# All four scatters of a slot wait for the last product of the next slot

## The chip, the core and the metric

The kernel runs on one core of a Trainium2 chip. The metric is the time of the whole program on the device, in microseconds (us), with everything between the inputs in HBM and the output in HBM. The core has five engines that run side by side, each through its own queue of instructions in order: TensorE (PE, matrix products; its weight loads are listed as PEld), VectorE (DVE), ScalarE (ACT), GpSimd (POOL) and SyncE (SP). Engines wait for each other through counters (semaphores): one engine raises a counter when an instruction is done, another waits until it has a certain value. SP here only issues transfers; POOL issues the indirect ones.

## The reference

One layer of a graph network with a residual and a layer norm, in float32:

```
x: 6250 x 128;  edges e = 0..99999, sorted by dst[e];  W: 384 x 128
h[e]   = concat(x[src[e]], x[dst[e]], edge_attr[e]) @ W + b
h[e]   = relu((h[e] - mean) / sqrt(var + 1e-5) * gamma + beta)
agg[n] = sum of h[e] over all edges with src[e] == n
out    = layernorm(x + agg)
```

The edges arrive sorted by `dst`, while the sum goes over `src`.

## The kernel before, in words

The 100,000 edges are cut into 782 tiles of 128 edges. Four tiles make a *slot* `q` (196 slots, loop at L1118). The kernel has two halves that overlap.

The first half computes, for each slot in the order of `dst`, the part of `h` that comes from the edge attributes and from `x[dst]`. `edges(s, q)` (L602) does it on PE: four products in float32 of the attributes with their weights (L611), then four products in bf16 that pick the `dst` rows out of a window of 42 nodes (L615); all go to one PSUM bank `hp`, of which there are two. `evict` (L619) copies the bank to SBUF on ACT, to one of eight buffers `hs` (L623), with the local number of the source node beside it (L624). Then POOL scatters each of the slot's four tiles to HBM with one indirect transfer (L641): every row of 128 values goes to its place in `sorted`, where the edges stand by blocks of source nodes. The places `place_i` were computed by counting, in work spread over earlier slots (`places`, L438).

The second half reads `sorted` back by pairs of blocks and adds the `x[src]` part, normalises and sums. The edges are divided into six splits (L38); a split is read back once all its scatters have landed, while the next split's slots run. A pair (class `Pair`, L719) passes through steps in fixed places of a flow (`FLOW`, L1063): SP loads it (`hl`, L715); DVE compares for the one-hot matrix (L733); PE turns that (L745) and ACT copies it (`ohn`, L749); ACT copies the loaded rows into PSUM (`sel`, L755); PE adds the picked rows of `x` to them (`pick`, L772); ACT squares and sums (L781) and takes the root (L784); DVE takes the reciprocal (L790) and scales (L796); PE sums by node (L805), and DVE adds that to the accumulator (L810). The last split is done by the class `Unit` (L819) after all slots, with the final layer norm.

The order on PE, DVE, ACT and SP is the order of the Python code (manual schedule, L973). In a slot it is: the loads for later slots, `edges(s, q)`, one step of the flow, `evict(s, q)`, a piece of `places`, the remaining steps of the flow, and then the scatters of the slot before. POOL's order is left to the scheduler of the framework; in the middle of the kernel POOL has nothing but scatters.

The scatters of slot `q - 1` are called at the end of slot `q` (L1144). From slot 13 to slot 194 they are *tied*: beside the wait for their `hs` buffer they wait for certain products of PE in slot `q`. For this, `pe()` (L99) notes the products of the slot as they are written, with their cost in columns (4 for float32, 1 for bf16): those of `edges`, of the turn, the pick and the sums, but not those of `places`. `scatters` (L630) then walks through the list and takes four of them: the products at which a quarter, a half, three quarters and all of the slot's cost are reached. Scatter `k` waits for the `k`-th of them. The scatters of the first 12 slots and of the last two are not tied.

Of the kernel before, what the change touches and what calls it, by code (L numbers as in the profile page):

```python
# [84 lines left out]
def fast_path(ctx, tc, io, bad_d, found):  # L85
# [10 lines left out]
    written = mybir.DependencyInfo(mybir.DependencyClass.Sync, mybir.DependencyReason.DATA)  # L96
# [91 lines left out]
    iota_p, zero_p, at = beside[:, 0:P], beside[:, P:P + 1], beside[:, P + 8:P + 8 + NB]  # L188
# [441 lines left out]
    def scatters(n, tied):  # L630

        total, seen, at = sum(c for _, c in done), 0, []
        for i, c in done:
            seen += c
            while len(at) < n and seen * n >= (len(at) + 1) * total:
                at.append(i)
        done.clear()
        for k, (s, q, j) in enumerate(waiting[:n]):
            t = q * PT + j
            parts = P if t < TILES - 1 else LAST  # L640
            i = nc.gpsimd.indirect_dma_start(  # L641
                out=sorted_d[s][:, :],
                out_offset=bass.IndirectOffsetOnAxis(ap=place_i[:parts, t:t + 1], axis=0),
                in_=hs_all[q % HS][:parts, j, :], in_offset=None,
            )
            if tied:
                tc.add_manual_dep(i.ins, at[k].name, written, reason="rows behind products")
            tc.declare_no_dep(i.ins, group=f"scatter{s}", reason="rows of different edges")
            tc.add_to_no_dep_group(f"scatter{s}", i.ins)
            if q < EARLY:  # L650
                tc.declare_no_dep(i.ins, group="clear", reason="see check_early")
                tc.add_to_no_dep_group("early", i.ins)
        del waiting[:n]
# [461 lines left out]
    for s, (n_tiles, _, _, _) in enumerate(SPLITS):  # L1115
        p0, p1 = first_tile[s] // PT, -(-first_tile[s + 1] // PT)
        slots = p1 - p0
        for i in range(slots):  # L1118
# [19 lines left out]
            if not TIE[0] <= q < TIE[1]:  # L1138
                scatters(len(waiting), False)
# [3 lines left out]
            if TIE[0] < q < TIE[1]:  # L1143
                scatters(len(waiting) - PT, True)  # L1144
# [359 lines left out]
```

## Time and profile before

| | |
|---|---|
| runs | 1376.14 us median of 3 (1372.72 to 1377.86) |
| the profiled execution | 1380.69 us, its span 1378.9 us |
| granted clock of PE, mean | 0.857 |
| PE | 975.2 us busy (71%) |
| DVE | 855.0 us busy (62%) |
| ACT | 773.5 us busy (56%) |
| POOL | 798.9 us busy (58%), of which 782 scatters 760.4 us |
| DMA | 247 MB, 179 GB/s over the span |

The span is the time from the first to the last instruction of the profiled execution. A row of the timeline begins with its start and its length in us; a bracket tells how long the engine had been idle before it and what ended that ("issue": nothing that the profile shows; "remote": a signal whose sender it can't name). A row of the groups by line has the busy time, the mean duration in ns, and the idle time before it. Starts and ends of matrix products are partly modelled, and a scatter's duration on POOL is that of its issue, not of the transfer.

### The profile page before, as it was taken

The numbers are of one execution on the slowest core, as the hardware profiler recorded it, in microseconds if no ns is written. First come the engines' busy times: TensorE is split into PE (matmuls) and PEld (weight loads), VectorE is DVE, ScalarE is ACT, GpSimd is POOL, SyncE is SP. The second block draws the span as 40 slices with busy tenths as digits, with TensorE's granted clock in tenths as the row PEclk, the third lists the DMA queues.
The fourth block names the chain that finished last, engine by engine and source line by source line (L and its number), as shares of the span: only waits on it lengthen the run. The fifth ranks groups of instructions, "written<-read, shape, count | busy, mean of one in ns | idle before, by whom it ended". The sixth has DMA issues, their size and how long they took to land. (4 is left out here: it accounts for less than half of the span.)

```text
span 1378.9 us, 27543 instructions
## 1 busy us (share of the span) xinstructions
PE 975.2 (71%) x8886; PEld 870.3 (63%) x8886; DVE 855.0 (62%) x2376; ACT 773.5 (56%) x3118; POOL 798.9 (58%) x835
## 2 busy tenths in 40 slices
PE   7457464345767676778777677778778787876895
PEld 5445453334666665777676667777778776765674
DVE  8573434524465656556575657678688867554797
ACT  4223232112555655564565557676778788665796
POOL 3656666666566665666565666566555555556054
PEclk9768687666888989878888899999999999988898
DMA  7758586455666655556656555665667655543332
GB/s 223 236 168 255 171 241 204 142 154 155 184 199 210 199 158 163 178 157 198 207 171 200 172 184 178 208 208 187 190 193 227 183 181 171 170 140 100 112 122 72
DMA packets 128052, 247.22 MB, mean 179 GB/s; under 512 B 47005, under 2 KB 61231, under 8 KB 127897
## 3 DMA queue, kind: packets, MB, share of 16 engines
q1 hardware_dynamic: 101924, 191.92, 46.8%
q0 software_dynamic: 25104, 53.05, 11.0%
q8 instruction: 71, 1.16, 0.4%
q14 instruction: 83, 0.68, 0.2%
q10 hardware_dynamic: 870, 0.40, 0.1%
HBM read 155.49 MB, written 89.80 MB: 178 GB/s over the span
## 5 line engine op out<-in xcount | busy, mean ns | idle before, releaser
L641 POOL DMA_INDIRECT sorted<-hs,place_i x782 | 760.4, 972 | 498.1 <-issue 210.6
L772 PE MATMUL sel<-xa,ohn 128*128 128x128 bf16 x2550 | 214.3, 232 | 174.9 <-issue 78.5
L781 ACT ACTIVATE sq<-sel 128x128 f32<-128x128 f32 x850 | 224.2, 280 | 158.9 <-PE sel L772 58.2
L772 PEld LDWEIGHTS <-ohn 128*128 128x128 bf16 x2550 | 174.8, 104 | 204.4 <-issue 174.7
L611 PE MATMUL hp<-w,eT 128*128 128x128 f32 x1564 | 258.3, 314 | 51.2 <-issue 37.9
L611 PEld LDWEIGHTS hp<-w,eT 128*128 128x128 f32 x1564 | 234.3, 225 | 83.2 <-issue 59.3
L805 PE MATMUL pa<-msg,ohe 128*128 128x130 f32 x1700 | 259.2, 308 | 24.1 <-issue 14.9
L623 ACT COPY hs<-hp 128x512 f32<-128x512 f32 x196 | 114.2, 583 | 288.7 <-issue 97.7
L805 PEld LDWEIGHTS pa<-msg,ohe 128*128 128x128 f32 x1700 | 236.4, 217 | 32.2 <-issue 19.0
L796 DVE SCALAR_TENSOR_TENSOR msg<-sel,rstd,cut 128x128 f32<-128x128 f32 x850 | 240.7, 345 | 8.0
L781 ACT ACTIVATION_READ_ACCUMULATOR sq<-sel 128x1 f32 x850 | 178.8, 210 | 0.0
L810 DVE TENSOR_TENSOR acc<-acc,pa 128x260 f32<-128x260 f32 x125 | 53.0, 424 | 201.0 <-PE pa L805 57.9
L733 DVE TENSOR_TENSOR ohe<-hl,beside 128x1024 f32<-128x1024 f32 (+2 forms) x125 | 131.4, 1052 | 23.3 <-PE sel L772 14.6
L749 ACT COPY ohn<-tr 128x1024 bf16<-128x1024 bf16 (+2 forms) x125 | 109.5, 876 | 37.9 <-PE pa L805 14.7
L755 ACT COPY sel<-hl 128x512 f32<-128x512 f32 (+1 forms) x225 | 127.9, 569 | 1.8 <-DVE msg L796 1.0
L599 DVE TENSOR_SCALAR ohd<-db,part_w 128x512 bf16<-128x512 bf16 x192 | 69.7, 363 | 72.1 <-remote 50.9
L615 PE MATMUL hp<-win,ohd 126*128 126x128 bf16 x782 | 88.5, 236 | 17.4 <-issue 15.4
L790 DVE RECIPROCAL rstd<-std 128x4 f32<-128x4 f32 (+1 forms) x225 | 38.6, 171 | 96.7 <-ACT std L784 45.2
L615 PEld LDWEIGHTS <-ohd 126*128 126x128 bf16 x782 | 69.0, 108 | 25.2 <-issue 20.9
L745 PE MATMUL tr<-ident_h,ohe 128*128 128x128 bf16 x850 | 75.5, 230 | 11.1 <-issue 9.4
L784 ACT ACTIVATE std<-ss,eps 128x4 f32<-128x4 f32 (+1 forms) x225 | 66.9, 297 | 7.3
L745 PEld LDWEIGHTS <-ohe 128*128 128x128 bf16 x850 | 57.7, 103 | 14.3 <-issue 14.2
(198 smaller groups left out, 1043.4 us busy)
## 6 DMA issues: line engine op xcount, KB each, us to landing
eT<-in_eT SPq DMA_DIRECT2D x96, 512.0 KB
hl<-sorted SPq DMA_DIRECT2D x75, 528.0 KB
db<-drel_d SPq DMA_DIRECT2D x96, 256.0 KB
sorted<-empty SPq DMA_DIRECT2D x100, 198.0 KB
hl<-sorted SPq DMA_DIRECT2D x50, 264.0 KB
sorted<-hs,place_i POOLq DMA_INDIRECT x782
hl<-sorted SPq DMA_DIRECT2D x25, 396.0 KB
sorted<-empty SPq DMA_DIRECT2D x50, 132.0 KB
```

The source lines that it names most:

```text
L611: pe(nc.tensor.matmul(hp[:, j, :], eT[:, at], w[:, 2, :], start=j == 0, stop=False, skip_group_check=True), 4)
L615: pe(nc.tensor.matmul(hp[:, j, :], oh[:3 * WN, at], win[:3 * WN, :], start=False, stop=j == m - 1, skip_group_check=True))
L623: nc.scalar.copy(hs[:, :m, 0:D], hp[:, :m, :])
L641: i = nc.gpsimd.indirect_dma_start(out=sorted_d[s][:, :], out_offset=bass.IndirectOffsetOnAxis(ap=place_i[:parts, t:t + 1], axis=0), in_=h ...
L733: nc.vector.tensor_tensor(self.ohe[:, :k, :], self.hl[:, :k, D:D + 1].to_broadcast([P, k, P]), row_bc(iota_p, k), op=ALU.is_equal)
L745: pe(nc.tensor.transpose(tr[:, j, :], half[:, j0 + j, 1::2], ident_h))
L749: nc.scalar.copy(self.ohn[:, :self.k, :], self.tr[:, :self.k, :])
L755: nc.scalar.copy(self.sel[g][:, :m, :], self.hl[:, j0:j0 + m, 0:D])
L772: pe(nc.tensor.matmul(sel[:, j, :], self.ohn[:, j0 + j, :], xa[:, b, i * D:(i + 1) * D], start=False, stop=j == m - 1 and i == 2, skip_gro ...
L781: nc.scalar.activation(sq[:, j, :], self.sel[g][:, j, :], AF.Square, accum_out=ss[:, j:j + 1])
L796: nc.vector.scalar_tensor_tensor(self.msg[:, j0 + j, 0:D], self.sel[g][:, j, :], rstd[:, j:j + 1], cut, op0=ALU.mult, op1=ALU.max)
L805: pe(nc.tensor.matmul(self.pa[:, h, :], self.ohe[:, j, :], self.msg[:, j, :], start=(j == h), stop=(j == k - 2 + h)), 4)
```

## The change

```
             if tied:
-                tc.add_manual_dep(i.ins, at[k].name, written, reason="rows behind products")
+                tc.add_manual_dep(i.ins, at[-1].name, written, reason="rows behind products")
```

Each of the four tied scatters of a slot now waits for the last product in the list, instead of the first for the product at a quarter, the second for that at a half, and so on. The last scatter waits for what it waited for before. In the built program, only the first of the four carries a wait for PE. The order of the instructions on PE, DVE, ACT and SP is the same as before. On POOL the scatters stand in the same order but for the last ten: the tied scatters of slot 193 stood mixed with those of slot 194, and now stand as a block of four behind the first three of slot 194. PE's products that raise its counter go from 1618 to 1086, since a product raises it only where something waits for it.

## The prediction

> **What bounds the kernel now.** I read the page first, then POOL's rows stage by stage, because the change touches POOL alone.
>
> ```profile
> span 1378.9 us, 27543 instructions
> PE 975.2 (71%) x8886; PEld 870.3 (63%) x8886; DVE 855.0 (62%) x2376; ACT 773.5 (56%) x3118; POOL 798.9 (58%) x835
> L641 POOL DMA_INDIRECT sorted<-hs,place_i x782 | 760.4, 972 | 498.1 <-issue 210.6
> ```
>
> No engine is full over the span. The 782 scatters take 760.4 us of POOL and leave 498.1 us of gaps between them. The table by stretches (columns: stretch, length, busy POOL time with the number of scatters, granted clock, DMA share, GB/s) gives the pace of a slot, which has four scatters:
>
> ```profile
> 100.00:275.00 175.00, 110.08 (x114) 0.73 0.68 204
> 275.00:540.00 265.00, 164.91 (x170) 0.83 0.57 178
> 540.00:810.00 270.00, 164.82 (x171) 0.83 0.58 180
> 810.00:1005.00 195.00, 117.42 (x121) 0.93 0.63 197
> 1005.00:1265.00 260.00, 145.41 (x151) 0.93 0.58 174
> ```
>
> Length over count times four: 6.14, 6.24, 6.32, 6.45 and 6.89 us a slot. POOL alone needs less. Its rows in time order show scatters back to back every 1.27 us (0.97 busy, 0.30 between), so 5.1 us a slot, and a longer gap where it waits. The waits of POOL in the last four stretches (in total us, times, longest) count those back-to-back gaps:
>
> ```profile
> POOL sorted L641 <- issue: 49.0, 124, 2.4
> POOL sorted L641 <- issue: 40.6, 118, 1.8
> POOL sorted L641 <- issue: 28.7, 77, 1.8
> POOL sorted L641 <- issue: 31.6, 76, 3.1
> ```
>
> What is left are stops: 170 - 124 = 46, then 53, 44 and 75, or 1.08, 1.24, 1.45 and 1.99 stops per four scatters. So POOL is close to setting the pace, and the question is why the others do not run ahead of it. The timeline of the last scatters, which are tied to nothing and run from 1263.10 to 1274.57 without a stop, shows it:
>
> ```profile
> 1263.10 0.97 POOL L641 DMA_INDIRECT sorted<-hs,place_i  x1 [0.40 <-issue]
> ...
> 1268.55 2.09 PE L805 MATMUL pa<-msg,ohe 128*128 128x130 f32 x8 [1.06 <-issue]
> ...
> 1274.57 0.87 POOL L641 DMA_INDIRECT sorted<-hs,place_i  x1 [0.30 <-issue]
> 1277.58 0.59 ACT L749 COPY ohn<-tr 128x512 bf16<-128x512 bf16 x1 [4.56 <-remote]
> 1277.70 0.43 DVE L810 TENSOR_TENSOR acc<-acc,pa 128x260 f32<-128x260 f32 x1 [7.93 <-remote]
> ...
> 1278.71 1.44 PE L772 MATMUL sel<-xa,ohn 128*128 128x128 bf16 x12 [8.07 <-ACT sel L755]
> ...
> 1285.25 0.43 DVE L810 TENSOR_TENSOR acc<-acc,pa 128x260 f32<-128x260 f32 x1 [0.18 <-PE pa L805]
> ...
> 1288.32 0.43 DVE L810 TENSOR_TENSOR acc<-acc,pa 128x260 f32<-128x260 f32 x1 [0.18 <-PE pa L805]
> ```
>
> PE finished the sums for DVE at 1270.64, and DVE got them at 1277.70, 2.3 us after the last scatter's end (1274.57 + 0.87); ACT's copy waited 4.56 us for an earlier product, and PE itself stood idle for 8.07 us behind ACT. Once the scatters are over, the same handover takes 0.18 us. So while scatters follow each other, the signal by which PE tells ACT and DVE of a finished product is **held**; it comes out in a stop of POOL. The same in the early stretch, timeline of slot 41:
>
> ```profile
> 259.92 0.39 PE L615 MATMUL hp<-win,ohd 126*128 126x128 bf16 x4
> ...
> 265.62 0.97 POOL L641 DMA_INDIRECT sorted<-hs,place_i  x1 [0.30 <-issue]
> ...
> 272.48 0.59 ACT L623 COPY hs<-hp 128x512 f32<-128x512 f32 x1 [13.52 <-issue]
> ...
> 273.12 2.08 PE L611 MATMUL hp<-w,eT 128*128 128x128 f32 x8 [12.82 <-ACT hs L623]
> ```
>
> ACT waits 13.52 us for a product that was done at 260.31, and PE 12.82 us for ACT. What one stop costs POOL, in mid-kernel:
>
> ```profile
> 639.42 0.97 POOL L641 DMA_INDIRECT sorted<-hs,place_i  x1 [0.30 <-issue]
> ...
> 641.70 0.96 POOL L641 DMA_INDIRECT sorted<-hs,place_i  x1 [1.30 <-PE hp L615]
> ```
>
> From the start of the last scatter of a row to the start of the next one it is 2.28 us instead of 1.27. That is the shortest kind of stop: the signals come out, and POOL goes on with them.
>
> **The change part by part.** No instruction of PE, DVE, ACT or SP moves, and no DMA is added or taken away.
>
> Removed: three of the four ties of a slot. Counted in the two built programs, 532 of PE's 1618 products that raise its counter no longer do, and POOL's queue has some 540 separate wait instructions fewer. A scatter that follows another takes 1.27 us from start to start in the untied run above as in the tied one, so the waits cost POOL nothing by themselves: 0.
>
> Added: the first scatter of a slot now waits for the last product of the next one. Behind it on POOL's queue stand only scatters, up to the tail. Who waits for those: ACT, to reuse the `hs` buffer eight slots later, some 50 us at 6.3 us a slot; and SP's first load of a sorted stretch.
>
> ```profile
> 279.15 1.00 POOL L641 DMA_INDIRECT sorted<-hs,place_i  x1 [0.30 <-issue]
> ```
> ```profile
> 297.48 0.00 SPq L715 DMA_DIRECT2D hl<-sorted  x1
> ```
> ```profile
> 1281.71 0.32 SPq L831 DMA_DIRECT2D hl<-sorted  x1
> ```
>
> The last scatter of the first split starts at 279.15, the load that needs it at 297.48. A scatter can slip by three back-to-back steps, 3.8 us; 18 us cover that: 0. At the end the last scatter starts at 1274.57 and the load that needs it at 1281.71. POOL's order of the last ten changes too: four tied ones now stand behind three untied ones, and may stop POOL once more. Between 0 and 3.8 us; half, 2 us.
>
> Moved: the stops. A slot is now four scatters in a row and one stop, with at least 3 x 1.27 + 2.28 = **6.09 us**, provided that PE has got through its whole slot when its signals come out. That is the lower end. In the five stretches it is worth -0.05, -0.15, -0.23, -0.36 and -0.80 us a slot. With 28.5, 42.5, 42.75, 30.25 and 37.75 slots that is -1, -6, -10, -11 and -30: **-58 us**.
>
> The other end: PE, ACT and DVE hand work to and fro inside a slot, and every handover from PE made during the four scatters comes out only at the stop. How far PE gets between two stops is in the counts above: one slot over 1.08, 1.24, 1.45 and 1.99 stops, so 0.93, 0.81, 0.69 and 0.50 of a slot a stop. The rest, 0.07, 0.19, 0.31 and 0.50, would follow after the stop with POOL waiting, where before POOL went on at once with its next quarter. A free slot takes about 5 us, an estimate: a pair of four blocks passes in 3.07 us when nothing is held (1285.25 to 1288.32), a slot has the work of 1.2 such pairs and 1.5 us of its own products. That adds 0.35, 0.95, 1.55 and 2.5 us to 6.09: 6.44, 7.04, 7.64 and 8.59, against before +0.20, +0.72, +1.19 and +1.70, times the slots +8, +31, +36 and +64: **+139 us**. The first stretch has no pairs yet, so its end stays at -1.
>
> Which value: between the ends, by the part of the rest that really remains. Less of it than the counts say, since a burst now starts with every signal of the slot before delivered (they come out in order, and the last is the one that POOL waits for), and since a third fewer signals queue up. But not nothing: ACT's queue holds the copy L623 of the new slot ahead of the copies that PE's next picks need, so one held signal stops a chain. I take half of the rest: (-57 + 139) / 2 = +41, with -1 and +2 **+42 us**. The profiled execution took 1380.7 us for its span of 1378.9; +42 makes 1423. It lies 4.6 us above the median of the runs, 1376.1, so the forecast is **1418 us**.
>
> **The rivals.** *Faster: one stop a slot is enough.* PE gets through its whole slot during the four scatters, and the time falls to 1376 - 58 + 2 = 1320. For it: in the early rows the scatter at 265.62 is the last of slot 39; POOL went on with the first half of slot 40, where the change makes it stop, and 2.28 us later, near 268, PE could have gone on and not at 273.12; and POOL stops once a slot instead of up to 1.99 times. Against it: in the last stretch half a slot a stop is all that PE makes. It decides where less than 0.25 of the rest remains (-57 + 0.25 x 196 = -8).
>
> *The full rest.* All of it remains: 1376 + 139 - 1 + 2 = 1516. For it, the counts as they stand; it belongs to the slower case and sets its far end.
>
> *Nothing is held.* The Trainium skill, page Perfetto Trace Analysis, section Tensor Engine Instruction, says that the profile's end of a matmul is computed from its size and not observed, and that the signal goes only when PSUM has acknowledged the writes. By that, the late signals would be PE's own late ends, POOL's bursts would hold nobody, a shift of at most 3.8 us with 18 us of cover would cost nothing, and the time would stay at 1376 to 1380. The trace speaks against it: PE's 8.07 us of idle time at 1278.71 has no matmul in flight, and the 0.18 us handovers come with the end of the scatters.
>
> **How the numbers follow.** About 0.5%, 7 us, is what a measurement of this kernel can tell from no change. The part of the rest is as good as unknown between 0 and 1. Below 0.25 the kernel is faster (chance 0.31), from 0.25 to 0.33 the same (0.06), above it slower (0.57); nothing held, 0.06, is the same as well. So faster 0.31, same 0.12, slower 0.57. The range leaves a tenth out at each end: 0.08 of the rest gives 1335, 0.88 gives 1492, rounded outward for the price of a free slot to 1335 to 1500.
>
> **What the changed profile would show.** POOL: runs of exactly four, so that about three in four scatters follow 0.30 us after another, and one stop a slot, before the first; its length tells the part: 1.3 us at the lower end, 2 to 3 us at my value. The stretches: 6.3 to 7.5 us a slot, worst after 1005. ACT's waits of 12 to 13.7 us at L623 gone, replaced by many of 3 to 5 us. The forecast is wrong if PE reaches its slot's last product while the scatters still run; then the stops are short, L623's idle time falls, and the kernel is faster.

## The result: 5.2% slower

The changed kernel takes 1443.65 us (median of 4 runs, 1441.36 to 1448.55), the kernel before 1374.43 us in the runs beside it (4 runs, 1371.8 to 1377.86). The ratio on record is 1.052, with a 95% interval of 1.049 to 1.055; the medians are 69 us apart, which by itself is 5.0%. Ratios are of fast runs alone; of all runs told here only one, of a kernel with a pause (1535.32 us), was slow and is left out. The forecast was 1418 us in a range of 1335 to 1500: the sign and the range hold, and the loss is 69 us in place of 42.

The page after has these lines for the span, the engines, the scatters and the two waits that show held signals (busy us, mean ns, then idle time before them); the last two lines are the same two waits in the kernel before:

```profile
span 1446.8 us, 27002 instructions
PE 993.8 (69%) x8886; PEld 880.9 (61%) x8886; DVE 852.9 (59%) x2376; ACT 771.0 (53%) x3118; POOL 799.2 (55%) x835
L641 POOL DMA_INDIRECT sorted<-hs,place_i x782 | 760.7, 973 | 564.3 <-issue 328.0
L623 ACT COPY hs<-hp 128x512 f32<-128x512 f32 x196 | 114.2, 583 | 355.4 <-remote 149.2
L810 DVE TENSOR_TENSOR acc<-acc,pa 128x260 f32<-128x260 f32 x125 | 52.9, 423 | 252.1 <-remote 117.9
```
```profile
L623 ACT COPY hs<-hp 128x512 f32<-128x512 f32 x196 | 114.2, 583 | 288.7 <-issue 97.7
L810 DVE TENSOR_TENSOR acc<-acc,pa 128x260 f32<-128x260 f32 x125 | 53.0, 424 | 201.0 <-PE pa L805 57.9
```

The scatters take what they took, 760 us; the gaps before them grew from 498.1 to 564.3 us, which is nearly all of the 67.9 us by which the span grew. To see where, the two kernels are cut at the same scatters: the first ones of slots 13, 42, 84, 126 and 156, and the last of all. The table by stretches of the kernel before, and then of the changed one (stretch, length, POOL's busy time with the scatters recorded, granted clock, DMA share, GB/s):

```profile
105.00:280.50 175.50, 112.74 (x117) 0.73 0.67 203
280.50:544.20 263.70, 163.09 (x169) 0.83 0.57 176
544.20:811.20 267.00, 163.61 (x168) 0.83 0.59 182
811.20:1006.30 195.10, 116.76 (x121) 0.94 0.63 196
1006.30:1274.60 268.30, 152.30 (x158) 0.93 0.57 171
```
```profile
103.60:278.00 174.40, 112.71 (x116) 0.74 0.66 204
278.00:557.40 279.40, 163.06 (x168) 0.78 0.54 170
557.40:844.80 287.40, 163.14 (x169) 0.81 0.55 170
844.80:1055.20 210.40, 116.46 (x120) 0.90 0.57 181
1055.20:1340.90 285.70, 152.94 (x157) 0.92 0.50 156
```

The differences are -1.1, +15.7, +20.4, +15.3 and +17.4 us. Before slot 13 it is -1.4 us (105.0 to 103.6), after the last scatter +1.6 us (104.3 to 105.9). The sum is 67.9, the whole difference of the spans. The loss begins at slot 42, where the pairs begin, and lies in every stretch from there. PE's granted clock fell as well (0.834 against 0.857 on average), and PE is busy for 18.6 us more; how much of this is a cause of the loss and how much follows from the stops, no run here separates.

What a stretch is made of can be counted in POOL's rows. Between the first scatters of slots 42 and 194 stand 608 steps from scatter to scatter, at 1.273 us each where nothing stops POOL: 774 us. The rest is stops, here taken as gaps of more than 0.55 us:

| | stops | beyond a plain step, each | sum | rows between stops |
|---|---|---|---|---|
| before | 208 | 1.02 us | 211 us | nearly all of one to five scatters |
| after | 112 | 2.51 us | 281 us | 72 of four, 33 of eight, few others |

Half as many stops, each two and a half times as long: +70 us. POOL's rows of the changed kernel, in mid-kernel (start, length, in brackets the idle time before):

```profile
641.72 0.97 POOL L641 DMA_INDIRECT sorted<-hs,place_i  x1 [6.57 <-ACT std L784]
642.99 0.97 POOL L641 DMA_INDIRECT sorted<-hs,place_i  x1 [0.30 <-issue]
...
650.63 0.97 POOL L641 DMA_INDIRECT sorted<-hs,place_i  x1 [0.30 <-issue]
654.24 0.97 POOL L641 DMA_INDIRECT sorted<-hs,place_i  x1 [2.64 <-issue]
...
658.06 0.97 POOL L641 DMA_INDIRECT sorted<-hs,place_i  x1 [0.30 <-issue]
660.84 0.96 POOL L641 DMA_INDIRECT sorted<-hs,place_i  x1 [1.81 <-issue]
```

Eight scatters in a row from 641.72 to 650.63, then 3.61 us to the next start; four, then 2.78 us. Over the 152 slots a stop after four takes 3.29 us from start to start, one after eight 4.96 us (means; the medians are 2.90 and 4.09). The timeline of one long stop tells what fills it:

```profile
668.42 0.27 PE L805 MATMUL pa<-msg,ohe 128*128 128x130 f32 x1 [1.05 <-issue]
...
669.12 0.29 PEld L805 LDWEIGHTS pa<-msg,ohe 128*128 128x128 f32 x1 [1.21 <-issue]
669.75 0.97 POOL L641 DMA_INDIRECT sorted<-hs,place_i  x1 [0.30 <-issue]
669.85 0.38 PE L805 MATMUL pa<-msg,ohe 128*128 128x130 f32 x1 [1.16 <-issue]
...
672.71 0.59 ACT L623 COPY hs<-hp 128x512 f32<-128x512 f32 x1 [8.56 <-remote]
...
673.28 0.59 ACT L755 COPY sel<-hl 128x512 f32<-128x512 f32 x1
...
673.93 1.44 PE L772 MATMUL sel<-xa,ohn 128*128 128x128 bf16 x12 [3.70 <-ACT sel L755]
...
675.16 1.06 PE L745 MATMUL tr<-ident_h,ohe 128*128 128x128 bf16 x8
...
676.97 0.97 POOL L641 DMA_INDIRECT sorted<-hs,place_i  x1 [6.25 <-ACT sq L781]
```

The eighth scatter in a row starts at 669.75. 2.96 us later ACT gets the signal that it had waited for during most of the row (8.56 us; the product that it needs was recorded as done at 662.93). PE's pick follows its copy, then the turn, and only then POOL goes on, 7.22 us after its last start. This is the rest of the slot, done while POOL waits.

PE itself doesn't run on undisturbed in the row. Its three instructions above carry no wait, and yet they start about 0.7 us apart, where shortly before (663.82) eight such products with their loads passed in 1.06 us. Over the whole kernel PE stands still for more than 0.3 us before an instruction that continues a group and carries no wait 184 times in the kernel before (105 us in total) and 233 times in the changed one (134 us). With plain DMAs in place of the scatters (below) it never does. So the scatters may hold up PE's work and not only its signals; as starts and ends of products are partly modelled, the traces don't tell the two apart. "Held" is said here of the handover from PE, whichever it is.

### The profile page after: what moved, and what is told of

Its sections match the earlier page's. It is cut to its first block, busy times and chain, and to the rows that moved or that the text cites. A ratio compares the mean times of both kernels' runs of the same rounds, so it can differ in the third digit from the quotient of the medians.

```text
span 1446.8 us, 27002 instructions
## 1 busy us (share of the span) xinstructions
PE 993.8 (69%) x8886; PEld 880.9 (61%) x8886; DVE 852.9 (59%) x2376; ACT 771.0 (53%) x3118; POOL 799.2 (55%) x835
## 5 line engine op out<-in xcount | busy, mean ns | idle before, releaser
L641 POOL DMA_INDIRECT sorted<-hs,place_i x782 | 760.7, 973 | 564.3 <-issue 328.0
L611 PE MATMUL hp<-w,eT 128*128 128x128 f32 x1564 | 265.8, 318 | 62.4 <-ACT hs L623 33.7
L623 ACT COPY hs<-hp 128x512 f32<-128x512 f32 x196 | 114.2, 583 | 355.4 <-remote 149.2
L772 PEld LDWEIGHTS <-ohn 128*128 128x128 bf16 x2550 | 181.5, 107 | 190.9 <-issue 162.7
L611 PEld LDWEIGHTS hp<-w,eT 128*128 128x128 f32 x1564 | 238.6, 228 | 91.3 <-issue 46.7
L805 PE MATMUL pa<-msg,ohe 128*128 128x130 f32 x1700 | 261.8, 305 | 45.9 <-issue 28.2
L805 PEld LDWEIGHTS pa<-msg,ohe 128*128 128x128 f32 x1700 | 234.4, 214 | 58.0 <-issue 37.1
L745 PE MATMUL tr<-ident_h,ohe 128*128 128x128 bf16 x850 | 83.1, 235 | 32.0 <-issue 31.4
L615 PE MATMUL hp<-win,ohd 126*128 126x128 bf16 x782 | 89.9, 239 | 16.6 <-issue 14.9
```

Of the source, the lines that this page charges most:

```text
L611: pe(nc.tensor.matmul(hp[:, j, :], eT[:, at], w[:, 2, :], start=j == 0, stop=False, skip_group_check=True), 4)
L615: pe(nc.tensor.matmul(hp[:, j, :], oh[:3 * WN, at], win[:3 * WN, :], start=False, stop=j == m - 1, skip_group_check=True))
L623: nc.scalar.copy(hs[:, :m, 0:D], hp[:, :m, :])
L641: i = nc.gpsimd.indirect_dma_start(out=sorted_d[s][:, :], out_offset=bass.IndirectOffsetOnAxis(ap=place_i[:parts, t:t + 1], axis=0), in_=h ...
L745: pe(nc.tensor.transpose(tr[:, j, :], half[:, j0 + j, 1::2], ident_h))
L772: pe(nc.tensor.matmul(sel[:, j, :], self.ohn[:, j0 + j, :], xa[:, b, i * D:(i + 1) * D], start=False, stop=j == m - 1 and i == 2, skip_gro ...
```

## The experiments

Two theories ran through them. H is the one of the prediction: signals are held while scatters follow each other, so the length of the row is what costs. L says that a later wait costs because it is later. The kernel before was measured anew beside each group of kernels, on the same chip; its median was 1357 to 1359 us there, but for one group, which is told with its run.

**The place of the one wait.** The four scatters together at another product:

```
-                tc.add_manual_dep(i.ins, at[-1].name, ...)
+                tc.add_manual_dep(i.ins, at[0].name, ...)     # e1_first
+                tc.add_manual_dep(i.ins, at[1].name, ...)     # e2_half
```

> All four scatters of a slot wait for the product at the first quarter of the next slot in place of the last one. Theory H (PE's signals are held while scatters follow each other, so what costs is four scatters in a row): POOL still runs in fours with one stop before the first, 6.6 to 7.3 us a slot after slot 42, 1425 to 1460 us, within 15 us of the changed kernel's 1444. Rival L (what costs is that POOL waits for a late product, whatever the row of scatters): the wait ends three quarters of a slot earlier, POOL's gap before the first scatter falls below 1.3 us, 1360 to 1390 us. Rival N (nothing is held): 1370 to 1380 us.

> All four scatters of a slot wait for the product at half of the next slot. H: as with the first quarter, 1425 to 1460 us and runs of four. L: between before and after, 1390 to 1415 us. N: 1370 to 1380 us.

Measured: 1417.11 us, ratio 1.044 (1.038 to 1.049), and 1423.95 us, ratio 1.048 (1.042 to 1.053). Both times lie just below the 1425 us from which H has them, in a group in which the kernel before was 16.5 us faster than in the first runs; L's ranges lie further off, the one by 27 us, the other by 9. A wait three quarters of a slot earlier takes back 0.9% of the 5.2%, and the intervals of the two ratios meet (the second measurement of the change, below, is 1.047). L falls: the place counts little, the row counts. The sum of the stops between slots 42 and 194 is 251 us for the first quarter and 269 us for the half, in rows of four (76 and 77) and eight (32 and 30).

**Rows of two.**

```
+                tc.add_manual_dep(i.ins, at[k | 1].name, ...)
```

> Two scatters wait for the product at half, two for the last one. H: the rows are half as long, so a stop delivers signals twice a slot; gaps of 1 to 1.5 us before the first and the third scatter, 0.30 us before the second and fourth; 1380 to 1425 us, between before and after. L: the last two scatters are as late as in the kernel before and the first two later by a quarter of a slot, which by L costs a sixth of the change (the quarters' delays are 3+2+1 in the change, 1+0+1 here, so a third at most): 1385 to 1400 us. N: 1370 to 1380 us.

Measured: 1385.26 us, ratio 1.022 (1.016 to 1.028). Both had this in their range, so it tells them apart no further, but it puts a point on the line: 165 stops of 1.32 us beyond a step, 218 us. The rows are of two (81), four (43) and six (36).

**No wait for products.**

```
-            if tied:
+            if False:
                 tc.add_manual_dep(i.ins, at[-1].name, ...)
```

> No scatter waits for a product at all; each waits for ACT's copy of its rows alone. H: POOL runs in fours or more, a stop comes only when ACT's copies run out, ACT waits longer at L623 for held signals, and the time is that of the changed kernel or above: 1430 to 1500 us. L: no wait for a product, so faster than before: 1330 to 1374 us. N: 1370 to 1380 us.

Measured: 1475.04 us, ratio 1.086 (1.081 to 1.092), the slowest of the kernels that differ only in their waits. The group of the scatters:

```profile
L641 POOL DMA_INDIRECT sorted<-hs,place_i x782 | 760.0, 972 | 593.9 <-ACT hs L624 360.3
```

POOL has the fewest waits and waits the most: 593.9 us, mostly for ACT's copies, 102 stops of 3.02 us beyond a step. A row starts the moment ACT's copy is there, right after a release, and holds PE's handovers before the others have done their part. L, which expects a gain, falls here altogether. One expectation of H missed: ACT's idle time at L623 did not grow, it fell to 266.4 us; the waits moved to POOL.

**The same rows without scatters.** SP writes each tile with a plain DMA, and POOL none:

```
-            i = nc.gpsimd.indirect_dma_start(out=sorted_d[s][:, :], out_offset=..., in_=hs..., )
+            nc.sync.dma_start(<128 rows of sorted, in the order of the tiles>, hs_all[q % HS][:parts, j, :])
```

> The rows of each tile are written by a plain DMA that SP issues, to rows in the order of the tiles and not to their sorted places (so the sums are over the wrong rows), and POOL issues no scatter at all; the same bytes go to the same tensors, and nothing waits for PE's products. H (POOL's issuing of scatters holds PE's signals): the signals come within some tens of ns at all times, as they do now where no scatter ran for 2.2 us (median 14 ns), the waits of ACT at L623 for signals go, and a slot goes down to 5.0 to 5.8 us from about 6.4: 150 to 250 us off the kernel before, ratio 0.82 to 0.90, if SP's queue keeps up. Rival D (the traffic of the written rows holds the signals, whoever issues it): signals still late by about 1 us, ratio 0.97 to 1.02. Rival N (nothing is held, the late signals are PE's own late ends): the same delays, ratio 0.97 to 1.02.

Measured: 1192.44 us, ratio 0.876 (0.872 to 0.879). D and N fall: the transfers are the same 247 MB, and the signals are on time. Of the 1083 products of PE that raise its counter, each changed it 13 to 15 ns after its end. The waits at L623 and DVE's for the sums (here L805) show it:

```profile
L623 ACT COPY hs<-hp 128x512 f32<-128x512 f32 x196 | 113.6, 580 | 125.3 <-issue 64.3
L805 DVE TENSOR_TENSOR acc<-acc,pa 128x260 f32<-128x260 f32 x125 | 52.3, 419 | 28.2 <-PE pa L800 27.9
```

**Which part of POOL's work.** The changed kernel, with plain DMAs issued by POOL in place of the scatters, same order, same waits:

```
-            i = nc.gpsimd.indirect_dma_start(...)
+            i = nc.gpsimd.dma_start(<128 rows of sorted, in the order of the tiles>, hs_all[q % HS][:parts, j, :])
             if tied:
                 tc.add_manual_dep(i.ins, at[-1].name, ...)
```

> The changed kernel with each scatter replaced by a plain DMA that POOL issues: the rows go to places in the order of the tiles, not to their sorted places (so the sums are over the wrong rows); the four of a slot wait for the last product of the next, as in the changed kernel. H as it stands (POOL's issuing of a DMA holds PE's signals, whatever the places): signals late while the DMAs follow each other, runs of four with a stop of 2 us or more, ratio to before 1.00 to 1.07 by the length that POOL takes for a plain one. Rival I (only the indirect form, with its scattered rows, holds them): signals within 15 ns as with SP's DMAs, ratio 0.86 to 0.95.

Measured: 1039.46 us, ratio 0.765 (0.763 to 0.767), below both. The page:

```profile
span 1036.9 us, 27189 instructions
PE 853.0 (82%) x8886; PEld 785.4 (76%) x8886; DVE 842.7 (81%) x2376; ACT 764.2 (74%) x3118; POOL 455.4 (44%) x835
L645 POOL DMA_DIRECT2D sorted<-hs x782 | 417.0, 540 | 505.7 <-ACT std L781 117.8
L623 ACT COPY hs<-hp 128x512 f32<-128x512 f32 x196 | 113.6, 580 | 89.9 <-PE hp L615 41.9
L807 DVE TENSOR_TENSOR acc<-acc,pa 128x260 f32<-128x260 f32 x125 | 52.5, 420 | 40.3 <-PE pa L802 40.2
```

Four plain DMAs in a row (0.54 us each) with one wait a slot, exactly the arrangement of the change, hold nobody: every signal of PE comes 13 to 15 ns after its product, during the rows too. So H as it stood, "POOL's issuing of a DMA", was too wide; it is the indirect form, with its scattered rows. The Trainium skill, page DMA: Bandwidth & Descriptors, section SWDGE vs HWDGE vs iDMA, puts direct and indirect DMAs of GpSimd on the same path, software on that engine that builds the descriptors. The shared path alone can't be what holds PE, then, since the plain ones don't. An indirect DMA with its rows in order was not run, so whether the form of the instruction or the scattered places do it stays open.

**A pause in the row.** A memset of about 1 us on POOL between the second and the third scatter:

```
+            if tied and k == 2:
+                nc.gpsimd.memset(pause, 0.0)     # 128x1024
             i = nc.gpsimd.indirect_dma_start(
```

> The changed kernel with one memset of 128x1024 on POOL (about 1 us, by the 0.195 us of a 128x128 one 1.0 to 1.6 us) between the second and the third scatter of a slot; all four still wait for the last product. H: the pause is a stop, signals come out in it, and the gap before the first scatter gets shorter by more than half of the pause: ratio to before 1.02 to 1.07, about the changed kernel's 1.05 in spite of 182 to 290 us more work on POOL. Rival B (POOL's own occupancy sets the pace, or any work on POOL holds the signals): 182 slots of 1.3 to 1.6 us more, 1444 + 240 to 290, ratio 1.2 to 1.27.

Measured: 1519.84 us (median of three), ratio 1.118 (1.112 to 1.124), between the two. The trace tells why it says nothing on them: POOL's order is left to the scheduler, which put the memsets far ahead of their scatters: 149 of the 182 ran before slot 42, where they filled POOL (8.05 us a slot from 13 to 42), the last of them at 505 us, and none stood in the rows after that, which were to be parted. It was made again with order dependencies that keep the memset in place:

```
+            rest = nc.gpsimd.memset(pause, 0.0) if tied and k == 2 else None
+            if rest:
+                tc.add_manual_dep(rest.ins, last.ins.name, follow, ...)   # order only
             i = nc.gpsimd.indirect_dma_start(
+            if rest:
+                tc.add_manual_dep(i.ins, rest.ins.name, follow, ...)
```

> As the pause before, but with the memset (0.96 us in that run) kept in its place between the second and the third scatter of a slot; without that, POOL's queue ran the memsets slots ahead, and most were over by slot 42. H: the pause is a stop; signals come out in it and the gap before the first scatter falls from 2 to 2.7 us by half a microsecond or more: ratio to before 1.03 to 1.09, that is at most 55 us over the changed kernel in spite of 200 us more between the scatters. Rival B (POOL's occupancy alone sets the pace): 182 slots of 0.96 + 0.15 us more, 200 us over the changed kernel, ratio 1.17 to 1.20.

Measured: 1369.57 us, ratio 1.008 (1.006 to 1.011). That is below B's range and also below H's: the pause gave back more than H said. The gap before the first scatter fell by 1.2 to 1.4 us a slot in the four stretches from slot 42 on. POOL has 176 us more to do than in the changed kernel, and the loss falls from 5.2% to 0.8%:

```profile
L646 POOL DMA_INDIRECT sorted<-hs,place_i x782 | 758.8, 970 | 319.3 <-issue 222.7
L643 POOL MEMSET pause<- 128x1024 f32 x182 | 176.4, 969 | 0.1
```

POOL's rows in time order show the pause at work, and a stop that has become short:

```profile
905.16 0.97 POOL L646 DMA_INDIRECT sorted<-hs,place_i  x1 [0.30 <-issue]
906.12 0.98 POOL L643 MEMSET pause<- 128x1024 f32 x1
907.26 0.97 POOL L646 DMA_INDIRECT sorted<-hs,place_i  x1 [0.17 <-issue]
908.54 0.97 POOL L646 DMA_INDIRECT sorted<-hs,place_i  x1 [0.30 <-issue]
910.95 0.97 POOL L646 DMA_INDIRECT sorted<-hs,place_i  x1 [1.45 <-issue]
```

Between slots 42 and 194 are 63 stops, 89 us beyond a step in all, and 152 pauses of 0.84 us beyond a step (a slot without a stop takes 5.93 us, four steps 5.09): 217 us, where the changed kernel stops for 281. B falls. Work that POOL does between scatters is worth more than the time that it takes, because it is no scatter. During the memsets PE's counter changes 1.14 times a microsecond, during the scatters (their first 1.27 us) 0.44 times: a memset lets PE's signals out.

**Other places for the four waits.** Starting from the kernel before:

```
-            while len(at) < n and seen * n >= (len(at) + 1) * total:
+            while len(at) < n and seen * 2 * n >= (2 * len(at) + 1) * total:    # e7_eighth
-                tc.add_manual_dep(i.ins, at[k].name, ...)
+                tc.add_manual_dep(i.ins, at[max(k - 1, 0)].name, ...)           # e8_quarter
```

> The kernel before with its four waits an eighth of a slot earlier: at 1/8, 3/8, 5/8 and 7/8 of the columns. H: single waits in four places as before, so the same stops, ratio 0.985 to 1.01. L (an earlier wait is a gain in itself; four waits at the first quarter took 0.9% less than four at the last): an eighth earlier gives 0.995 to 1.00.

> The kernel before with its waits a quarter earlier: at 1/4, 1/4, 1/2 and 3/4 of the columns. H: the first two scatters form a row of two and the others stay single; between the kernel before and the pairs (1.022): 1.00 to 1.02. L: 0.98 to 0.995.

Measured: 1362.23 us, ratio 1.002 (1.000 to 1.003), and 1381.19 us, ratio 1.015 (1.012 to 1.019). The first is no change and tells H and L little apart; the second is as H has it and against L: three of its waits come a quarter earlier, none later, and it is slower, for its first two scatters now form a row.

**The pause with the early wait**, to see whether the two gains add up to a kernel faster than before: the kernel with the pause, its `at[-1]` replaced by `at[0]`.

> The kernel with the memset kept between the second and the third scatter, and all four scatters waiting for the product at the first quarter of the next slot in place of the last. By the runs so far (the pause took the changed kernel from 1.052 to 1.008; the first quarter in place of the last took it from 1.052 to 1.044) both together give 0.995 to 1.005 if they add up. If the pause has already taken what the earlier wait gains, 1.005 to 1.01.

Measured: 1264.45 us, and the kernel before 1120.34 us (9 runs, 1118.25 to 1123.05), ratio 1.129 (1.127 to 1.131). The kernel before is far below every other time of its own, on a chip on which it had taken 1359 us a quarter of an hour earlier. The trace kept is that of the kernel with the pause, and in it the scatters hold nothing:

```profile
span 1263.2 us, 27184 instructions
L646 POOL DMA_INDIRECT sorted<-hs,place_i x782 | 759.0, 971 | 218.9 <-issue 169.1
L623 ACT COPY hs<-hp 128x512 f32<-128x512 f32 x196 | 114.4, 583 | 336.1 <-DMA sorted<-hs,place_i 273.8
```

The scatters are issued at the same pace as ever (971 ns), the program is that of the pause but for one index, yet the handovers are prompt. Where DVE stood idle for PE's sums, and these ended less than 1.3 us after a scatter's start, it began 0.04 us after their end in all 38 cases; in the profile of the pause alone it was more than 0.2 us late in 23 of 30. Nor does PE stand still in the middle of a group here. POOL runs without a stop at 5.92 to 5.93 us a slot, and ACT waits for it at L623. There the pause is a plain loss: 182 slots of 0.84 us are 153 us, and 144 were measured. That the kernel before held nothing either is argued from its time and this sum. Neither expectation was about this; whether the two gains add up stays open.

**The change once more**, to see what it costs where nothing is held:

> The changed kernel once more, beside new runs of the kernel before. In the last runs the kernel before took 1120 us where it had taken 1352 to 1378 in all others, and in the profile taken with them the signals of PE came 14 ns (median) and 41 ns (mean) after the products while the scatters ran. So there are executions in which the scatters hold no signals. Where the kernel before takes 1120 here too: H says that the change costs next to nothing, since PE's slots are shorter than POOL's 5.1 us and nobody is held, ratio 0.99 to 1.02, POOL back to back through the middle. A rival W (the later wait costs POOL a stop a slot, held signals or not) says 1.04 to 1.07. Where the kernel before takes 1350 to 1380 again, both say 1.045 to 1.06, and what changes between the two kinds of executions stays open.

Measured: 1423.06 us, the kernel before 1357.69 us, ratio 1.047 (1.043 to 1.052). So the signals were held again, and the result is repeated: 107 stops of 2.48 us beyond a step, in rows of four (62) and eight (38). What the change costs where nothing is held was not seen.

No kernel tried here beats the kernel before and still puts the rows in their places; the waits at odd eighths equal it.

## Why the prediction was right, and where it was not

**What bounds the kernel: right.** Stops of POOL, and in them the release of held signals. With plain DMAs in their place the time falls to 1039 us on the same queue with the same waits, and the waits at L623 and for the sums fall from 288.7 and 201.0 us in the kernel before to 89.9 and 40.3. Where DVE stood idle for PE's sums (L805) in the kernel before, and these ended less than 1.3 us after a scatter's start, it began more than 0.2 us late in 24 of 36 cases (median 1.21 us); with plain DMAs in none of 17.

The prediction had PE's signals alone, and that holds for what can be seen. The records of the counters seem to say more: of signals due less than 1.3 us after a scatter's start, the next recorded change comes more than 0.2 us later for 82% of PE's, 48% of ACT's and 52% of DVE's. But with scatters many changes have no record (in the kernel before ACT's 1251 have 735, DVE's 1783 have 1051, PE's 1618 have 1470; with plain DMAs all have one), so the next record isn't the signal. Whoever waits tells it better. DVE's reciprocal needs ACT's root, and in all 75 cases in which DVE stood idle for it, 60 of them less than 1.3 us after a scatter's start, it began 0.03 us after the root's end:

```profile
1245.33 0.97 POOL L641 DMA_INDIRECT sorted<-hs,place_i  x1 [0.30 <-issue]
...
1246.06 0.30 ACT L784 ACTIVATE std<-ss,eps 128x4 f32<-128x4 f32 x1
1246.38 0.18 DVE L790 RECIPROCAL rstd<-std 128x4 f32<-128x4 f32 x1 [1.97 <-ACT sq L781]
...
1246.61 0.97 POOL L641 DMA_INDIRECT sorted<-hs,place_i  x1 [0.30 <-issue]
```

One reading of the prediction was off by a little: some of the waits that it took for back-to-back gaps ("issue") were stops. Counted by gaps over 0.55 us, its four stretches have 44, 49, 44 and 72 stops in place of 46, 53, 44 and 75.

**Removed waits, and the slip of scatters, at 0: consistent with the sum.** The plain step stayed at 1.27 us, the stretch up to slot 42 lost nothing, and ACT's waits for a landed scatter, 34.7 us in total at L623 in the kernel before, are 34.7 us in the changed one. The tail was given 2 us and took 1.6: the last ten scatters run as a block without a stop and hold PE's signals. ACT gets its signal 2.49 us after the last one has been issued (1340.92 + 0.87), after 9.46 us of waiting, and PE's pick had stood for 12.91:

```profile
1340.92 0.87 POOL L641 DMA_INDIRECT sorted<-hs,place_i  x1 [0.30 <-issue]
1344.28 0.59 ACT L749 COPY ohn<-tr 128x512 bf16<-128x512 bf16 x1 [9.46 <-remote]
...
1345.41 1.44 PE L772 MATMUL sel<-xa,ohn 128*128 128x128 bf16 x12 [12.91 <-ACT sel L755]
```

**The early stretch, -1 us: right**, -1.1 from slot 13 to 42.

**Moved stops: the step that failed is the size of a stop.** The prediction had +1, +10.5, +12.5 and +17 us for the last four stretches (half of the way between its ends); +15.7, +20.4, +15.3 and +17.4 were measured. The last two are near it, the first two are far above, and the first is above even its upper end of +8. Two terms did that. First, "a slot is now four scatters in a row and one stop" holds for two thirds of the rows only: 33 of 112 are rows of eight. A release that lets PE pass the last products of two slots, so that POOL has both to run, would make them; this is argued. The rows of eight are in the first two of these stretches above all (27 of them between slots 42 and 126). Second, the shortest stop, 2.28 us, was read off a single stop (at 641.70). On average a stop grows with the row: in the kernel before 2.06 to 2.33 us after one to three, 2.50 after four; in the changed one 3.29 after four and 4.96 after eight. The row is not all of it: after four scatters the same row costs 0.8 us more in the changed kernel. There one wait stands for the slot's last product, and a whole chain (ACT's copies, pick, turn) runs behind the release, as in the timeline at 669.75. That is the rest of the prediction, reckoned from the number of stops a slot before, and its size was wrong where a slot had about one stop. Of the way from the lower end to the upper, the prediction took half in every stretch; measured were 1.55, 0.74, 0.56 and 0.50 of it.

**The rivals.** *One stop is enough* fell: the stops became as few as it says, and fewer, but each took 2.51 us beyond a step. *Nothing is held* fell by the plain DMAs: at the same traffic and the same order of instructions on PE the late signals are gone. The Trainium skill, page Perfetto Trace Analysis, section Tensor Engine Instruction, says that a matmul's end is computed and not observed. The computed end by itself doesn't make the delays, since with plain DMAs they are 13 to 15 ns throughout. That PE's real ends are late while scatters run is not excluded. *The full rest* was the far side and remained that: 281 us of stops where it would have needed some 350 (211 + 139).

**What was to be seen.** Three in four scatters 0.30 us after another: 641 of 782, more, for the rows of eight. The stop before the first scatter, 2 to 3 us at the value taken: 1.83 to 2.56 us of gap by stretch, slots without a stop counted in. The stretches 6.3 to 7.5 us a slot, worst after 1005: 6.65, 6.84, 7.02 and, from slot 156 to 194, 7.35. Wrong was that ACT's waits of 12 us and more at L623 would go. The longest is now this:

```profile
309.10 0.59 ACT L623 COPY hs<-hp 128x512 f32<-128x512 f32 x1 [14.32 <-issue]
```

It ends just after a row of twelve scatters (291.54 to 305.56), of a length that the prediction didn't have.

## What to carry to other kernels

Where an engine's work holds up another while it runs without a break, the waits that break it up are part of the schedule: count the rows and the stops, and price a stop by the length of the row ahead of it and by the work that is due behind it. Here half as many stops cost a third more, and a microsecond of idle work put into each row gave nearly all of it back. Gathering waits at one point is safe only where the engine that waits is harmless when it runs on.

## What was not expected of the hardware

- While POOL issues indirect DMAs one after the other (0.97 us each, 1.27 us from start to start), PE's products reach ACT and DVE late, and PE stands still in the middle of groups; in a stop PE's first recorded signal comes 1.8 to 2.8 us after the last start (medians by stretch, both kernels). Signals of ACT to DVE came on time in the same rows (0.03 us, 60 of 60 in the kernel before). While POOL issues plain DMAs of the same bytes (0.54 us each), PE's signals come in 13 to 15 ns. Holding and the longer issue together are worth 319 us of 1358 here (ratio 0.765), and the granted clock that went with it was 0.939 in place of about 0.855.
- Plain DMAs from SP gave 1192 us, the same ones from POOL 1039, with the waits of the changed kernel; what SP's longer queue costs was not looked into.
- The holding isn't there in every execution: in one of the five groups of measurements the same kernel before took 1120 us in place of 1357 to 1359. What makes the difference is open. Every run here was recorded by the profiler (each has its span and granted clock), and counter changes lack records where PE is held; so a part of the recording in the holding isn't excluded. Where nothing is held POOL's own pace, 5.1 us a slot without a stop, would be the bound (an estimate from the plain step of 1.27 us), and a change of the kind tried here would have to be judged anew.
